# Reordering the opening, the scales and the down weights' unpacking in the first job of a fused FFN, S4, FFN kernel

## The chip, the cores and the metric

The kernel runs on one core of a Trainium2 chip. The core has a matrix engine (TensorE, PE in the profile), a vector engine (VectorE, DVE), a scalar engine (ScalarE, ACT), GpSimd (POOL) and SyncE (SP), which here only issues transfers (DMAs). Each engine has its own list of instructions and works it off in order; engines wait for each other through semaphores. The metric is the device time of one execution in microseconds (us), lower is better: the median of several executions.

## The reference

The input is 2048 tokens of width HID = 1024, as (2, 1024, 1024). Three residual layers follow each other, each after a layer norm: half of an FFN, an S4 convolution along the sequence, and half of the same FFN once more.

```python
def _dequant(qweight, scales, qzeros, g_idx):
    shifts = jnp.arange(PACK, dtype=jnp.uint32) * BITS
    qw = qweight.astype(jnp.uint32)
    w = (qw[:, None, :] >> shifts[None, :, None] & MAXQ).reshape(-1, qweight.shape[1])
    qz = qzeros.astype(jnp.uint32)
    z = ((qz[:, :, None] >> shifts[None, None, :] & MAXQ) + 1).reshape(qzeros.shape[0], -1)
    s = scales[g_idx]
    return (w.astype(scales.dtype) - z[g_idx].astype(scales.dtype)) * s
...
xf = x.reshape(-1, x.shape[-1])
h = jax.nn.silu(xf @ Wg) * (xf @ Wu)
out = h @ Wd
...
x = x + 0.5 * ffn(layernorm(x))
x = x + s4(layernorm(x))
x = x + 0.5 * ffn(layernorm(x))
```

Wg and Wu are 1024 x 2752, Wd is 2752 x 1024. All three are stored as 4-bit numbers, eight to a 32-bit word, with one scale and one zero point for every 128 rows (a group) of a column.

## The kernel before

**Jobs.** The tokens are cut into four blocks of 512. A job is one FFN on one block; there are eight (JOBS), and the S4 layer of two blocks is woven into the jobs between. A job has a gate-and-up half (`gate_up`) and a down half (`down`). Only job 0 unpacks weights: it turns the 4-bit words into signed bytes less their zero points, writes these bytes to memory (w_q for gate and up, wd_q for down), and all later jobs read them back.

**Gate and up.** The 21.5 blocks of 128 hidden columns are taken in 8 waves: waves 0 to 4 of three blocks, waves 5 to 7 of two, the last with the half block too. A wave has 8 steps, one for each group g of 128 input rows, so there are 64 steps. A step multiplies one tile of weights by the block's normalised, transposed input. Each product is made twice, with the rounded high part xTh (fp32r) and with the small rest xTl (f16) (L857): 12 matmuls a step in waves 0 to 4, 8 in waves 5 and 6, 10 in wave 7. The sums pg stay in PSUM; between two groups each is multiplied by the quotient of the two groups' scales, rat (`scaled`; ScalarE L813, VectorE L817). So a matmul of group g+1 waits for the rescale of its own sum. After a wave's last group, `gated` makes g = silu (ScalarE L889), hf = up times g (VectorE L892, three buffers in hfpool), and `halves` splits hf into hh and hl (POOL L898, L899). The halves of wave 0 are put off: they are kept in the list `put_off` and taken in wave 1, at g > 4.

**Down.** 44 steps, two halves of 512 output columns with 22 hidden blocks each, 8 matmuls a step (L951), with a rescale between hidden blocks (L813, L817).

**A weight's way in job 0.** `fetch` and `fetch_zeros` load packed words and zero points (SyncE, L563, L570); `split` runs `signed_bytes` on VectorE (L624, L628, L631); `dequantize` copies eight planes out as bytes q (POOL L669, for wave 1 also ScalarE L667); `keep_bytes` stores them (SyncE L675); `load_bytes` reads a step's tile b back (SyncE L774, 4 steps ahead); `make_weights` casts it to w_up (POOL L790, some on ScalarE L788, 3 steps ahead). The down weights go the same way in six blocks (`fetch_down`, `split_down`, `dequantize_down` POOL L703, `keep_bytes_down` SyncE L711, `load_bytes` L781).

**The opening.** The first tile has no time for the way through memory: `first_split` unpacks wave 0, `dequantize_first` writes its eight planes j as bytes q (odd by POOL L605, even by ScalarE L607), and each plane is copied straight into the first tile b (L608). `keep_first` stores the planes to w_q (L612). The zero points of all of gate and up are unpacked into ztab (`zero_points_in_pieces`, L351, L360) and stored as z_dram (L380), from which `fetch_zeros` reads. The first block's rows xn are normalised by `first_rows` (ScalarE L1815, VectorE L1817) and transposed by `first_turn` (TensorE L1830, ScalarE L1832, VectorE L1833; three of eight through POOL L1837, L1838).

**Scales.** `scale_rows` loads rows of scales (SyncE L399); `scales_in_pieces` transposes them (TensorE L414), copies them out (ScalarE L422), makes them safe against zeros (POOL L425 to L427), takes reciprocals (VectorE L429) and multiplies the quotients rat (POOL L433, L434). This is done for blocks 0 to 2 in the opening, 3 to 8, 9 to 14 and from 15 on in the steps that a list gives.

**What sets the order.** Work that doesn't belong to a step's matmuls hangs on hooks: `at(up, s, f)` has f written before the matmuls of step s of gate and up, or in their middle if s ends in .5; `at(dn, d, f)` the same for the down. `in_pieces` hands a sequence's parts to a list of steps. `pinned` and `in_order_of_writing` fix the written order on the engines named; elsewhere a scheduler may shift instructions within what dependencies allow. All of SyncE's transfers are in one list and leave in order.

Of the kernel before, what the change touches and what calls it, by code (L numbers as in the profile page):

```python
# [57 lines left out]
def macaron_s4_kernel(  # L58
# [314 lines left out]
    def zero_points_in_pieces(which, z):  # L373

        p, n = z.shape
        zi, tab = (t2(f"{a}_{which}").bitcast(I32)[:p, : 8 * n] for a in ("zi", "ztab"))
        yield from unpacked_zeros_in_pieces(tab, z, zi)
        yield
        dst, seg = (zd_dram, SEGD) if which else (z_dram, SEG)
        nc.sync.dma_start(dst.rearrange("g (s n) -> (g s) n", s=seg), tab)  # L380

# [202 lines left out]
    def first_split(zq):  # L584
# [15 lines left out]
        def dequantize(j):  # L600
            pair = pairs.setdefault((j % 2, j // 4), t2(f"q_0_{j}").bitcast(I8)[:, : 2 * n])
            q = pair.rearrange("p (a n) -> p a n", a=2)[:, j // 2 % 2, :]
            view = lambda a, dt: a.bitcast(dt).rearrange("p (n k) -> p k n", k=4)[:, j // 2, :]
            if j % 2:
                nc.gpsimd.tensor_copy(q, view(raw, I8))  # L605
            else:
                nc.scalar.activation(q, view(even, U8), AF.Identity, bias=minus_128)  # L607
            nc.sync.dma_start(first_tile[j:P:8], q[: P // 8])  # L608

# [105 lines left out]
    def first_weights(up, dn, at):  # L715
# [17 lines left out]

        def when(n):
            if n < 12:
                return up, s0 + n
            return dn, n - 14 if n >= 24 else n - 12 if n > 15 else (0, 0, 1, 2)[n - 12]

        def soon(n):
            hooks, s = when(n)  # L740
            return hooks, s + 0.5

        for n in range(6 * 8):
            k, j = divmod(n, 8)
            a, rt = divmod(k, 3)
            if j == 0:
                at(*when(max(0, n - 7)), lambda a=a, rt=rt: fetch_down(a, rt))
                steps = [when(max(0, n - d)) for d in (4, 3, 3, 2, 1, 0)]
                if n == 8:
                    steps = [(up, s0 + d) for d in (3.5, 4, 5, 5.5, 6.5, 7.5)]  # L750
                if n == 16:
                    steps = [(dn, d) for d in (1, 1.5, 2, 2.5, 3, 4)]
                in_pieces(at, steps, lambda a=a, rt=rt: split_down(a, rt))
            at(*when(n), lambda a=a, rt=rt, j=j: dequantize_down(a, rt, EVEN_FIRST[j]))
            if j % 2:
                at(*soon(n), lambda a=a, rt=rt, j=j: keep_bytes_down(a, rt, j // 4, j // 2 % 2))

# [25 lines left out]
    def make_weights(i):  # L783
        j, stage, s = queue[i]
        b = loaded.pop(i)
        made[i] = t = wpool.tile(list(b.shape), F32R, tag="w", name=f"w_{stage}_{j}_{s}")
        if j == 0 and stage == "up" and s % GK in ((), (5, 6, 7), (1, 2, 5))[(s > 7) + (s > 23)]:
            nc.scalar.copy(t, b)  # L788
        else:
            nc.gpsimd.tensor_copy(t, b)  # L790
# [28 lines left out]
    def gate_up(j, b, hooks):  # L819
        hi, lo = pieces[b]  # L820
        ps = {}
        for s, (wi, g) in enumerate(STEPS):
            if wi == 1 and g > 4 and put_off:
                put_off.pop(0)()
# [62 lines left out]
    def gated(j, f, pg, pu):  # L887
# [12 lines left out]

        if j == 0 and f in WAVES[0]:
            put_off.append(halves)
# [696 lines left out]
    def fast():  # L1599
# [5 lines left out]
        for j, (b, k) in enumerate(JOBS):  # L1605
# [88 lines left out]
            if j == 0:  # L1694
                rows = {}
                for s, f in ((0, lambda: next(points, None)), (0, lambda: fetch_zeros(1)), (1, lambda: fetch(2)), (2, lambda: fetch_zeros(2))):
                    at(up, s, pinned(f, ET.SP))
                for first_use, s, k0, k1 in ((5, 1, 3, 9), (14, 6, 9, 15), (30, 11, 15, WIDE)):
                    load = lambda k0=k0, k1=k1: rows.update({k0: scale_rows(k0, k1)})
# [8 lines left out]
                for c in range(1, NC):  # L1708
                    more = lambda c=c: first_turn(c)
                    at(up, {1: 0.5, 2: 0.5, 4: 2.5}.get(c, c - 2), pinned(more, *STARTING, ET.PE))  # L1710
                at(up, 1, pinned(lambda: first_rows(2, 512, HID), ET.DVE))
                first_weights(up, dn, at)
# [7 lines left out]
            if after:  # L1720
                ab, ak = after
                if ak == 1:
                    at(up, 55 if j == 0 else 6, lambda: load_x(ab, rows_of(u, ab)))
                    if j == 0:
                        steps = [(dn, 4 + (3 * i) / 2) for i in range(8)] + [(dn, 15.5), (dn, 16)]
                        in_pieces(at, steps, lambda: moments_by_tile(ab, 1, True, LIFT))
                        steps = [(dn, 17 + i / 2) for i in range(10)]
                        in_pieces(at, steps, lambda: deviations_in_pieces(ab, 1))
# [117 lines left out]
    def start():  # L1846
# [21 lines left out]
        dequantize_first(2)  # L1868
        next(second)
        next(first_scales)  # L1870
        guess(0, 1, mv, LIFT)
        for _ in first_scales:
            pass
        keep_first(1, 0, nc.gpsimd)
        dequantize_first(4)
        dequantize_first(6)
        keep_first(0, 0, nc.sync)
        keep_first(1, 1, nc.gpsimd)
        keep_first(0, 1, nc.scalar)
        keep_warm(10, scratch)  # L1880
# [15 lines left out]
        first_rows(3, P, 512)  # L1896
        for t in (0, 1, 3):
            first_rows(t, 512, HID)
        keep_warm(6)
        return points, zeros_down  # L1900

    points, zeros_down = in_order_of_writing(start, *STARTING, ET.PE, ET.Pool)
    x.pop(0)
# [87 lines left out]
```

## Time and profile before

| | us |
|---|---|
| median of 3 executions | 2038.86 (2038.42 to 2038.87) |
| the profiled execution | 2038.82 |
| its span, first to last instruction | 2036.9 |
| first matmul of gate and up, job 0 | starts 19.19 |
| gate and up of job 0 (64 steps) | 19.19 to 191.60 |
| down of job 0 (44 steps) | 191.60 to 280.72 |
| gate and up of job 3 (no unpacking, no S4 work) | 806.67 to 962.26 |
| down of job 3 | 962.26 to 1040.64 |

The profile is of one execution. Times count from the first instruction. An instruction's line gives its start, its length, engine, line of the kernel and operation, with output and input (partitions x elements); at the end in brackets, how long the engine had been idle before it, and who released it. "x3" at the end means three like instructions in a row. SPq, ACTq are instructions that issue transfers. The granted clock (PEclk) is the share of full speed at which TensorE was allowed to run. Since job 3 runs the same matmuls with nothing to unpack, it serves as the measure of job 0's stages. The time of a step is taken from the start of its first matmul to that of the next step's first.

### The profile page before, as it was taken

The numbers are of one execution on the slowest core, as the hardware profiler recorded it, in microseconds if no ns is written. First come the engines' busy times: TensorE is split into PE (matmuls) and PEld (weight loads), VectorE is DVE, ScalarE is ACT, GpSimd is POOL, SyncE is SP. The second block draws the span as 40 slices with busy tenths as digits, with TensorE's granted clock in tenths as the row PEclk, the third lists the DMA queues.
The fourth block names the chain that finished last, engine by engine and source line by source line (L and its number), as shares of the span: only waits on it lengthen the run. The fifth ranks groups of instructions, "written<-read, shape, count | busy, mean of one in ns | idle before, by whom it ended". The sixth has DMA issues, their size and how long they took to land.

```text
span 2036.9 us, 29679 instructions
## 1 busy us (share of the span) xinstructions
PE 2005.1 (98%) x9202; PEld 1373.4 (67%) x9202; DVE 1627.9 (80%) x2710; ACT 1416.2 (70%) x2221; POOL 1372.1 (67%) x1771
## 2 busy tenths in 40 slices
PE   7999999999999999999999999999999999999998
PEld 4555776577766677665876578667686676866576
DVE  8888878868888787878778777887878878777776
ACT  7888787747775576777767776764776646767775
POOL 6878868748765577756976578754687636965542
PEclk9999999999999999999999999999999999999999
DMA  4344332243524227411562126242163331661113
GB/s 159 104 121 132 110 88 76 68 105 85 154 74 98 79 62 202 121 30 35 135 171 83 33 50 169 81 94 82 47 158 98 81 89 39 159 192 36 34 36 103
DMA packets 345965, 197.13 MB, mean 97 GB/s; under 512 B 166989, under 2 KB 323670, under 8 KB 345798
## 3 DMA queue, kind: packets, MB, share of 16 engines
q1 hardware_dynamic: 344382, 192.74, 34.9%
q10 hardware_dynamic: 1288, 2.01, 0.3%
q8 instruction: 75, 1.23, 0.3%
q14 instruction: 92, 0.75, 0.1%
q0 software_dynamic: 128, 0.39, 0.1%
HBM read 127.52 MB, written 48.57 MB: 86 GB/s over the span
## 4 chain that ended last, share of the span: by engine, by line
PE 93%; DVE 3%; ACT 2%; issue 1%; POOL 1%; DMA 1%; SPq 0%; ACTq 0%; DVEq 0%; POOLq 0%
PE pg L857 57%; PE po L951 30%; PE pc L1319 3%; PE pb L1319 1%; ACT pg L813 1%; DVE pg L817 1%; DVE po L817 0%; DVE rawd L628 0%; POOL w_up L790 0%; DMA x<-in_L_attn_u_dram 0%; DVE hf L892 0%; POOL hl L899 0%; DMA b<-wq 0%; POOL hh L898 0%; PE pt L239 0%
## 5 line engine op out<-in xcount | busy, mean ns | idle before, releaser
L813 ACT ACTIVATE pg<-pg,rat 128x512 f32<-128x512 f32 x1280 | 807.0, 661 | 387.1 <-PE pg L857 383.2
L817 DVE TENSOR_TENSOR pg<-pg,rat 128x512 f32<-128x512 f32 x1128 | 747.8, 692 | 150.7 <-PE pg L857 143.8
L857 PE MATMUL pg<-xTh,w_up 128*128 128x512 f32 x2752 | 845.5, 435 | 6.3 <-DVE pg L817 2.5
L857 PE MATMUL pg<-xTl,w_up 128*128 128x512 f16 x2752 | 708.9, 382 | 4.8 <-DVE pg L817 2.4
L857 PEld LDWEIGHTS pg<-xTh,w_up 128*128 128x128 f32 x2752 | 518.7, 189 | 170.4 <-ACT pg L813 6.9
L790 POOL CAST w_up<-b 128x768 fp32r<-128x768 int8 (+2 forms) x491 | 375.3, 770 | 362.5 <-PE pg L857 259.1
L813 ACT ACTIVATE po<-po,ratd 128x512 f32<-128x512 f32 x669 | 437.9, 662 | 143.3 <-PE po L951 142.7
L951 PE MATMUL po<-hl,w_down 128*128 128x512 f32 x1344 | 526.6, 393 | 1.6 <-DVE po L817 1.4
L951 PE MATMUL po<-hh,w_down 128*128 128x512 f32 x1344 | 521.3, 390 | 0.0
L817 DVE TENSOR_TENSOR po<-po,ratd 128x512 f32<-128x512 f32 x611 | 423.7, 696 | 112.8 <-PE po L951 112.3
L857 PEld LDWEIGHTS <-w_up 128*128 128x128 bf16 x2752 | 226.9, 98 | 342.8 <-issue 158.4
L790 POOL CAST w_down<-bd 128x512 fp32r<-128x512 int8 x352 | 219.0, 625 | 145.0 <-PE po L951 71.9
L951 PEld LDWEIGHTS po<-hl,w_down 128*128 128x128 f32 x1344 | 251.9, 188 | 64.5 <-DVE po L817 6.1
L951 PEld LDWEIGHTS po<-hh,w_down 128*128 128x128 f32 x1344 | 252.4, 188 | 50.6
L899 POOL TENSOR_TENSOR hl<-hf,hh 128x512 fp32r<-128x512 f32 x168 | 218.5, 1300 | 6.5
L898 POOL CAST hh<-hf 128x512 fp32r<-128x512 f32 x168 | 107.3, 639 | 81.4 <-DVE hf L892 62.6
L892 DVE SCALAR_TENSOR_TENSOR hf<-pg,rat,g 128x512 f32<-128x512 f32 x168 | 121.0, 746 | 40.5 <-ACT g L889 34.7
L889 ACT ACTIVATE g<-pg,rat 128x512 f32<-128x512 f32 x168 | 110.1, 687 | 33.7 <-PE pg L857 17.5
L1004 POOL TENSOR_TENSOR x<-x,yr 128x512 f32<-128x512 f32 x52 | 66.9, 1286 | 0.0
L291 POOL TENSOR_TENSOR lo<-x,hi 128x512 f16<-128x512 f32 x48 | 62.3, 1298 | 0.0
L189 DVE BATCH_NORM_STATS2 stats<-x 128x6 f32<-128x512 f32 x88 | 59.9, 680 | 0.0
L289 POOL TENSOR_TENSOR mid<-hi,top 128x512 bf16<-128x512 f32 x48 | 56.1, 1169 | 0.0
(214 smaller groups left out, 1079.2 us busy)
## 6 DMA issues: line engine op xcount, KB each, us to landing
b<-wq SPq DMA_DIRECT2D x319, 96.0 KB
bd<-wdq SPq DMA_DIRECT2D x336, 64.0 KB
x<-in_L_attn_u_dram SPq DMA_DIRECT2D x30, 512.0 KB
yz<-y SPq DMA_DIRECT2D x56, 256.0 KB
yr<-yz SPq DMA_DIRECT2D x56, 256.0 KB
b<-wq SPq DMA_DIRECT2D x128, 64.0 KB
sz<-xn SPq DMA_DIRECT2D x16, 512.0 KB
st<-sz SPq DMA_DIRECT2D x64, 128.0 KB
```

Source lines behind the costliest of these rows:

```text
L291: nc.gpsimd.tensor_tensor(lo[:, own], n[:, own], hi[:, own].bitcast(F32), ALU.subtract)
L790: nc.gpsimd.tensor_copy(t, b)
L813: nc.scalar.activation(dst, src, AF.Copy, scale=sc)
L817: nc.vector.tensor_tensor(dst, src, sc.to_broadcast(list(dst.shape)), ALU.mult)
L857: product = lambda: nc.tensor.matmul(p, weights, (lo, hi)[k][:, g, :], start=(g == 0 and not done), stop=(g == GK - 1 and done), skip_grou ...
L889: nc.scalar.activation(g, pg, AF.Silu, scale=rat[:, 2 * f, GK - 1 :])
L892: nc.vector.scalar_tensor_tensor(hf, pu, last, g, ALU.mult, ALU.mult)
L898: nc.gpsimd.tensor_copy(hi, hf)
L899: nc.gpsimd.tensor_tensor(lo, hf, hi.bitcast(F32), ALU.subtract)
L951: nc.tensor.matmul(ps[c], w[:, bass.ts(c, P)], part, start=(f == 0 and k == 0), stop=(f == NF - 1), skip_group_check=True,)
L1004: nc.gpsimd.tensor_tensor(part, part, rows_back.pop((a, t)), ALU.add)
L1319: nc.tensor.matmul(dst, lhsT, rhs, start=start, stop=stop, skip_group_check=True)
```

## The change

1. Opening: the plane j = 6 of the first tile and the table z_dram are sent by ScalarE instead of SyncE, the table at the end of `start` instead of in step 0; both odd planes are stored by POOL before it makes the first quotients; the second half of wave 1's packed words is fetched after the stores of the even planes; the rows xn of tile 2 are normalised within `start` and no longer in step 1.
2. Scales of blocks 3 to 8 are made from step 4 (before: 5), those of blocks 9 to 14 from step 6 (before: 14), with their rows loaded in steps 0 and 1 (before: 1 and 6).
3. `make_weights`: the casts of ScalarE at s % 8 in (1, 2, 5) begin with s > 31 instead of s > 23.
4. The halves of blocks 0 to 8 are put off instead of those of 0 to 2, and taken at g > 4 in waves 1, 2 and 3.
5. The down's six blocks are fetched, split, copied and stored at steps written in one table. A number d is step 52 + d of gate and up below 12, and step d - 12 of the down from there.
6. In the down of job 0, the statistics of the next block's rows and their deviations are taken at other steps.

No instruction is added or removed on any engine; two transfers change the engine that issues them. Jobs 1 to 7 are as before.

```diff
--- before.py
+++ after.py
@@ -376,8 +376,8 @@
         zi, tab = (t2(f"{a}_{which}").bitcast(I32)[:p, : 8 * n] for a in ("zi", "ztab"))
         yield from unpacked_zeros_in_pieces(tab, z, zi)
         yield
-        dst, seg = (zd_dram, SEGD) if which else (z_dram, SEG)
-        nc.sync.dma_start(dst.rearrange("g (s n) -> (g s) n", s=seg), tab)
+        dst, seg, queue = (zd_dram, SEGD, nc.sync) if which else (z_dram, SEG, nc.scalar)
+        queue.dma_start(dst.rearrange("g (s n) -> (g s) n", s=seg), tab)
 
     def inverse(*what):
         for _ in inverse_in_pieces(*what):
@@ -605,7 +605,8 @@
                 nc.gpsimd.tensor_copy(q, view(raw, I8))
             else:
                 nc.scalar.activation(q, view(even, U8), AF.Identity, bias=minus_128)
-            nc.sync.dma_start(first_tile[j:P:8], q[: P // 8])
+            queue = nc.scalar if j == 6 else nc.sync
+            queue.dma_start(first_tile[j:P:8], q[: P // 8])
 
         def keep(odd, half, queue):
             rows = w_q[0].rearrange("(r b a two) n -> two b r a n", b=2, a=2, two=2)[odd, half]
@@ -731,29 +732,26 @@
                 at(up, s0 + o, lambda w=w, odd=odd: keep_bytes(w, odd))
         s0 = len(STEPS) - 12
 
-        def when(n):
-            if n < 12:
-                return up, s0 + n
-            return dn, n - 14 if n >= 24 else n - 12 if n > 15 else (0, 0, 1, 2)[n - 12]
-
-        def soon(n):
-            hooks, s = when(n)
-            return hooks, s + 0.5
-
-        for n in range(6 * 8):
-            k, j = divmod(n, 8)
+        def when(d):
+            return (up, s0 + d) if d < 12 else (dn, d - 12)
+
+        blocks = (
+            (-3, (-1, -0.5, 0, 0.5, 1, 1.5), (1, 1, 2, 3, 4, 5, 6, 7)),
+            (1, (3.5, 4, 5, 5.5, 6.5, 7.5), (8, 9, 10, 11, 12, 12, 13, 14)),
+            (9, (13.5, 15, 16.5, 17.5, 19, 19.5), (18, 18, 18.5, 19, 20, 20, 21, 21.5)),
+            (15, (20.5, 22, 23.5, 24, 25, 25.5), (24.5, 24.5, 25, 25.5, 26, 26.5, 27, 27.5)),
+            (22, (27, 28.5, 30, 31, 31.5, 32.5), (31.5, 31.5, 32, 32.5, 33, 33.5, 34, 34.5)),
+            (29, (35, 37, 39, 39.5, 41, 41.5), (40, 40.5, 41, 41.5, 42, 42.5, 43, 43.5)),
+        )
+        for k, (fetched, split_at, copied) in enumerate(blocks):
             a, rt = divmod(k, 3)
-            if j == 0:
-                at(*when(max(0, n - 7)), lambda a=a, rt=rt: fetch_down(a, rt))
-                steps = [when(max(0, n - d)) for d in (4, 3, 3, 2, 1, 0)]
-                if n == 8:
-                    steps = [(up, s0 + d) for d in (3.5, 4, 5, 5.5, 6.5, 7.5)]
-                if n == 16:
-                    steps = [(dn, d) for d in (1, 1.5, 2, 2.5, 3, 4)]
-                in_pieces(at, steps, lambda a=a, rt=rt: split_down(a, rt))
-            at(*when(n), lambda a=a, rt=rt, j=j: dequantize_down(a, rt, EVEN_FIRST[j]))
-            if j % 2:
-                at(*soon(n), lambda a=a, rt=rt, j=j: keep_bytes_down(a, rt, j // 4, j // 2 % 2))
+            at(*when(fetched), lambda a=a, rt=rt: fetch_down(a, rt))
+            in_pieces(at, [when(d) for d in split_at], lambda a=a, rt=rt: split_down(a, rt))
+            for i, (j, d) in enumerate(zip(EVEN_FIRST, copied)):
+                at(*when(d), lambda a=a, rt=rt, j=j: dequantize_down(a, rt, j))
+                if i % 2:
+                    half = lambda a=a, rt=rt, i=i: keep_bytes_down(a, rt, i // 4, i // 2 % 2)
+                    at(*when(d + 0.5), half)
 
 
     LOAD, MAKE = 4, 3
@@ -784,7 +782,7 @@
         j, stage, s = queue[i]
         b = loaded.pop(i)
         made[i] = t = wpool.tile(list(b.shape), F32R, tag="w", name=f"w_{stage}_{j}_{s}")
-        if j == 0 and stage == "up" and s % GK in ((), (5, 6, 7), (1, 2, 5))[(s > 7) + (s > 23)]:
+        if j == 0 and stage == "up" and s % GK in ((), (5, 6, 7), (1, 2, 5))[(s > 7) + (s > 31)]:
             nc.scalar.copy(t, b)
         else:
             nc.gpsimd.tensor_copy(t, b)
@@ -820,7 +818,7 @@
         hi, lo = pieces[b]
         ps = {}
         for s, (wi, g) in enumerate(STEPS):
-            if wi == 1 and g > 4 and put_off:
+            if wi in (1, 2, 3) and g > 4 and put_off:
                 put_off.pop(0)()
             if j == 0 and s < 8:
                 w = in_order_of_writing(next_weights, ET.SP)
@@ -898,7 +896,7 @@
             nc.gpsimd.tensor_copy(hi, hf)
             nc.gpsimd.tensor_tensor(lo, hf, hi.bitcast(F32), ALU.subtract)
 
-        if j == 0 and f in WAVES[0]:
+        if j == 0 and f < WAVES[3][0]:
             put_off.append(halves)
         else:
             halves()
@@ -1693,9 +1691,9 @@
                         at(up, 13 + t, pinned(lambda t=t: store(t), ET.SP))
             if j == 0:
                 rows = {}
-                for s, f in ((0, lambda: next(points, None)), (0, lambda: fetch_zeros(1)), (1, lambda: fetch(2)), (2, lambda: fetch_zeros(2))):
+                for s, f in ((0, lambda: fetch_zeros(1)), (1, lambda: fetch(2)), (2, lambda: fetch_zeros(2))):
                     at(up, s, pinned(f, ET.SP))
-                for first_use, s, k0, k1 in ((5, 1, 3, 9), (14, 6, 9, 15), (30, 11, 15, WIDE)):
+                for first_use, s, k0, k1 in ((4, 0, 3, 9), (6, 1, 9, 15), (30, 11, 15, WIDE)):
                     load = lambda k0=k0, k1=k1: rows.update({k0: scale_rows(k0, k1)})
                     at(up, s, lambda load=load: in_order_of_writing(load, ET.SP))
                     steps = [(up, first_use + i / 2) for i in range(4)]
@@ -1708,7 +1706,6 @@
                 for c in range(1, NC):
                     more = lambda c=c: first_turn(c)
                     at(up, {1: 0.5, 2: 0.5, 4: 2.5}.get(c, c - 2), pinned(more, *STARTING, ET.PE))
-                at(up, 1, pinned(lambda: first_rows(2, 512, HID), ET.DVE))
                 first_weights(up, dn, at)
             if j == 1:
                 tables = s4_tables()
@@ -1722,9 +1719,9 @@
                 if ak == 1:
                     at(up, 55 if j == 0 else 6, lambda: load_x(ab, rows_of(u, ab)))
                     if j == 0:
-                        steps = [(dn, 4 + (3 * i) / 2) for i in range(8)] + [(dn, 15.5), (dn, 16)]
+                        steps = [(dn, d) for d in (2.5, 4, 6, 9, 10.5, 14.5, 16, 17.5, 18.5)]
                         in_pieces(at, steps, lambda: moments_by_tile(ab, 1, True, LIFT))
-                        steps = [(dn, 17 + i / 2) for i in range(10)]
+                        steps = [(dn, 21 + i / 2) for i in range(4)]
                         in_pieces(at, steps, lambda: deviations_in_pieces(ab, 1))
                     else:
                         steps = [(up, s) for s in range(12, 21)] + [(up, 20.5)]
@@ -1866,17 +1863,17 @@
         first_scales = scales_in_pieces(0, 3, srow)
         next(first_scales)
         dequantize_first(2)
-        next(second)
         next(first_scales)
         guess(0, 1, mv, LIFT)
+        for _ in range(2):
+            keep_first(1, _, nc.gpsimd)
+        dequantize_first(4)
+        dequantize_first(6)
+        keep_first(0, 1, nc.scalar)
+        keep_first(0, 0, nc.sync)
+        next(second)
         for _ in first_scales:
             pass
-        keep_first(1, 0, nc.gpsimd)
-        dequantize_first(4)
-        dequantize_first(6)
-        keep_first(0, 0, nc.sync)
-        keep_first(1, 1, nc.gpsimd)
-        keep_first(0, 1, nc.scalar)
         keep_warm(10, scratch)
         keep_warm(10, scratch)
         bias = small.tile([P, NT], F32, tag="bias", name="bias")
@@ -1894,12 +1891,14 @@
         for _ in range(5):
             next(points)
         first_rows(3, P, 512)
-        for t in (0, 1, 3):
+        for t in range(NT):
             first_rows(t, 512, HID)
+        for _ in points:
+            pass
         keep_warm(6)
-        return points, zeros_down
-
-    points, zeros_down = in_order_of_writing(start, *STARTING, ET.PE, ET.Pool)
+        return zeros_down
+
+    zeros_down = in_order_of_writing(start, *STARTING, ET.PE, ET.Pool)
     x.pop(0)
     fast()
     x.clear()
```

## The prediction

> **What bounds the kernel now.** I read the busy table first, then the slices, then the matmuls' windows stage by stage, then the waits and the timeline where a stage is longer than its twin.
>
> ```profile
> span 2036.9 us, 29679 instructions
> PE 2005.1 (98%) x9202; PEld 1373.4 (67%) x9202; DVE 1627.9 (80%) x2710; ACT 1416.2 (70%) x2221; POOL 1372.1 (67%) x1771
> PE   7999999999999999999999999999999999999998
> ```
>
> TensorE is busy for 98% of the span, and no matmul is removed; only its idle or slow time can be won. The change touches job 0 alone, so its stages are set against job 3, which issues the same matmuls without unpacking weights. Columns: stretch, its length, PE busy, granted clock, DMA share, GB/s. The first five rows are job 0's waves 0, 1, 2, 3 and 4, 5 to 7; the sixth is job 3's whole gate and up; the last three are job 0's down in two halves and job 3's down.
>
> ```profile
> 19.19:48.54 29.35, 25.25 (x97) 0.94 0.41 129
> 48.54:71.14 22.60, 22.06 (x98) 1.00 0.48 142
> 71.14:96.32 25.18, 22.54 (x97) 1.00 0.32 100
> 96.32:140.96 44.64, 43.65 (x193) 1.00 0.33 93
> 140.96:191.60 50.64, 49.30 (x208) 1.00 0.52 160
> 806.67:962.26 155.59, 155.36 (x688) 1.00 0.25 75
> ...
> 191.60:234.93 43.33, 41.91 (x169) 1.00 0.36 106
> 234.93:280.72 45.79, 42.99 (x177) 1.00 0.29 87
> 962.26:1040.64 78.38, 78.38 (x344) 1.00 0.55 138
> ```
>
> From the first matmul of one step to that of the next, a clean step of 12 matmuls takes 2.70 us (most steps of the trace), one of 8 takes 1.80, one of 10 takes 2.25; so the five stretches of job 0's waves would take 21.6, 21.6, 21.6, 43.2 and 46.8 (16 x 1.80 + 8 x 2.25) if clean. Excess: 7.8, 1.0, 3.6, 1.4, 3.8 us, 17.6 in all (172.4 against job 3's 155.6 gives 16.8). The down takes 89.1 against 78.4: 10.7, of which some 5 are 48 transposes of about 0.1 us each on TensorE. Before all this lie 19.19 us until the first matmul. What is there to win is some 20 us, 1% of the span. Its sharpest pieces, by single steps and by TensorE's waits:
>
> ```profile
> 15.49 2.66 DMA b<-q
> 18.31 0.83 POOL w_up L790
> 19.19 2.97 PE pg L857 x6
> ...
> 26.35 1.65 DVE L1817 TENSOR_SCALAR xn<-x,mv,r 128x512 f32<-128x512 f32 x1
> 29.12 0.59 PE L857 MATMUL pg<-xTl,w_up 128*128 128x512 f16 x2 [1.17 <-DVE pg L817]
> ...
> 71.21 0.75 DVE L429 RECIPROCAL safe<-safe 128x96 f32<-128x96 f32 x1 [1.71 <-POOL safe L427]
> 73.54 1.15 PE L857 MATMUL pg<-xTh,w_up 128*128 128x512 f32 x3 [0.91 <-DVE hf L892]
> ...
> 86.48 2.22 SPq L774 DMA_DIRECT2D b<-wq  x5
> 88.98 0.83 ACT L788 CAST w_up<-b 128x768 fp32r<-128x768 int8 x1 [2.19 <-PE pg L857]
> 90.42 0.95 PE L857 MATMUL pg<-xTl,w_up 128*128 128x512 f16 x3 [1.53 <-ACT pg L813]
> ```
>
> Read as four stories. (1) The first weights wait for the last plane's copy. (2) Step 2 (4.90 us) stops for a rescale queued behind xn. (3) Step 16 (4.06) stops because VectorE idles 1.71 for the scales' reciprocal while hf waits behind it. (4) Step 21 (4.40) stops because ScalarE waits 2.19 for bytes that SyncE asked for only at 86.48; the first of its stores of q (L675) had begun at 73.54, and each waits for POOL's copies, queued behind the splits hh and hl (0.6 and 1.28 us each).
>
> **What the Trainium skill says.** "SBUF — State Buffer", Terms, has VectorE and GpSimd arbitrate for a shared port pair, an exclusive lock held for the whole instruction. The trace agrees: xn takes 0.54 us at 19.75 and 1.65 at 26.35, beside POOL's xTl (26.43, 1.28). "DMA: Bandwidth & Descriptors", Issuing engines are not separate DMA queues: another issuing engine saves only the sequencer's time. Here that time is 0.5 to 0.6 us an issue, against 2.66 to landing. "TensorE: Matmul & The Clock Gate", Part 1 (the HAM clock gate), lets the clock follow a free-running activity window; wave 0's 0.94 is the trace's half clock, 19.10 to 22.52. Engine queue depths in the same page: ScalarE and VectorE are strict FIFO, as stories 2 to 4 show.
>
> **The change part by part** (gains positive).
>
> Opening. Plane 6 left SyncE at 15.49, because a fetch of raw_1 (0.58, at 14.23) and plane 4 stood ahead; its values were ready at 14.24. Now ScalarE issues it at about 14.3 and SyncE issues plane 4 at 14.23, the fetch coming after the stores. At 2.66 the landing is 16.96 instead of 18.15. POOL must be free: r to 14.5, two store issues 1.70, rat 0.55, so 16.75. First matmul about 18.0, 1.2 earlier. ScalarE's issue of the zero table waits for ztab (19.84) with the first rescale queued behind it; 19.84 + 0.45 = 20.3 against the 20.2 at which that rescale would come: 0.1 lost. The half-clock stretch costs about 1.7 of the 3.4 us. If the window's edge stays at 22.52, up to 0.6 more time is spent at half clock; if the earlier start brings the edge forward, up to 1.5 is won. I take 1.1; bounds 0.5 and 2.5.
>
> Steps 1 to 8. xn of tile 2 goes from step 1 to a place where it takes 0.54 before any rescale: the 1.17 stall goes, and what is late next is the rescale itself; 0.45 to 1.3. Against it, the next scales' chain comes into wave 0: reciprocal 0.75 on VectorE, and on POOL two preparations of 0.3 to 0.4 and two rat of 0.3 to 0.4, with six transposes (0.54 on PE, only moved). VectorE was busy for 10.00 of 10.00 us between 40 and 50, so at step 8 the mirror of story 3 can cost 0.3 to 1.0 or, if its POOL input is early, nothing. Net +0.7; bounds -0.5 and +1.5.
>
> Step 16. The reciprocal and its wait of 1.71 are gone from the border; hf comes straight after its silu. All 1.36 of excess: +1.3 (0.7 to 1.36).
>
> Steps 20 to 24. Halves of blocks 3 to 8 are taken at steps 21 to 23 and 29 to 31 instead of at the wave border, so POOL's q copies come up to six instructions (3 x (0.6 + 1.28) = 5.6 us) earlier, SyncE's stores with them, then the five loads behind them. Casts 25 and 26 also leave ScalarE, and 30 and 31 go to it (0.83 each). The excess of 1.70 at step 21 and 0.5 in 22 and 23: +2.0 (0.8 to 2.2). Its cover: hfpool has three buffers, so hf of the next wave waits for hl of this one, which is now written in the last three steps of the wave.
>
> Blocks of the down. Block 0 spread over up 51 to 53.5: +0.3 (0 to 0.6). Block 2's split used VectorE to the brim in the first four down steps; columns: stretch, its length, VectorE busy:
>
> ```profile
> 191.60:203.00 11.40, 11.26 (x16) 1.00 0.15 41
> 203.00:214.00 11.00, 10.03 (x20) 1.00 0.30 88
> ```
>
> Those steps are 1.91, 2.43, 2.45 and 2.49 instead of 1.82: 2.0 us. The same six pieces (L624, L628, L631; 5.5 us) now lie between steps 1.5 and 7.5, but three statistics (0.68 each) come to steps 2.5 to 6 as well: +1.5 (0.5 to 2.1). Blocks 3 to 5 move by one to seven steps and the deviations from 17 to 21; steps 10 to 20 have an excess of 3.3, largest at 16, 18 and 19 (2.39, 2.62, 2.41) where all these met. VectorE's work stays: +1.0 (0 to 2.5). Steps 22 to 43, where transposes are the excess: 0 (±0.4).
>
> Sum: 1.1 + 0.7 + 1.3 + 2.0 + 0.3 + 1.5 + 1.0 = 7.9. Stalls new to places I have no row for (hf's buffers, step 8) I take at 0.4. Gain 7.5. The profiled execution took 2038.82 (span 2036.9 and 1.9 around it), the median of the runs is 2038.86: the same to 0.04. Forecast 2038.8 - 7.5 = **2031.3**, own range 2028.5 to 2034.
>
> **The rivals.** (a) VectorE is the bound where it matters and its work only moves: the down's and early gains (0.7 + 1.5 + 1.0 + 0.3) vanish, and half a microsecond more in the stretch 40 to 60. Left: 1.1 + 1.3 + 2.0 - 0.5 = 3.9, so 2034.9. For it: 10.00 of 10.00 between 40 and 50. Against it: after 203 VectorE has idle time to take the pieces. (b) Upper bounds meet: 2.5 + 1.5 + 1.36 + 2.2 + 0.6 + 2.1 + 1.5 = 11.8, so 2027.0; the early clock edge decides. (c) Slower: the put-off halves hold hf's three buffers. At steps 24 and 32 the last hf of a wave needs hl popped only one step before; POOL (9.92 busy of 10.00 between 50 and 60) need only be more than about 2 us behind, and VectorE, in order, stops with all rescales behind it, then TensorE without free banks. A backlog of 8 us at each of the two new borders costs 2 x (8 - 2) = 12 us and eats the gain: 2038.8 - 7.5 + 12 = 2043.3. It decides from about 6 us of backlog; against it, wave 1 already worked so, and step 16's stall there was the reciprocal's. (d) The change doesn't reorder what it says: then no change, 2038.8; but the lists are explicit, and it is counted in (a).
>
> **How the numbers follow.** Forecast 0.56, (a) with (d) 0.20 over 2033.5 to 2039, (b) 0.20 over 2025.5 to 2028.5, (c) 0.04. A measurement can tell about 0.2%, 4.1 us, from no change: 2034.8 is the edge. Faster: 0.56 + 0.20 + 0.08 of (a) = 0.84; same 0.12; slower 0.04. The range 2027.3 to 2035.5 leaves out about 0.10 of (b), 0.05 of (a) and (c).
>
> **What would show it.** Right: first gate matmul at about 18.0; step 2 under 4.2; step 16 and step 21 at 2.7 to 3.0; SyncE's loads before step 21 some 5 us earlier; down steps 2 to 4 near 1.9. Wrong: VectorE waiting for POOL's hl before hf at steps 24 and 32; a stall over 1 us at step 8; the half clock lasting beyond 22.5; or statistics bringing the stalls to steps 5 to 8.

## The result, and the profile after

The changed kernel takes 2036.41 us (median of 22 executions, 2031.42 to 2038.60), the kernel before 2039.26 in the same sessions (22 executions, 2037.72 to 2040.71). The ratio over all executions is 0.9983, with a 95% interval of 0.9976 to 0.9989: 3.5 us faster (2.2 to 4.9); the two medians differ by 2.9. Forecast were 7.5 us and a range that ends at 2035.5. The direction was right, the size less than half of what was forecast, and the time lies outside the range. The executions are not evenly spread: 5 of the 22 took 2031.4 to 2033.0, the other 17 took 2035.2 to 2038.6. The profiled one (2036.95) belongs to the upper group; none of the lower group was profiled. The experiments trace the loss to one place in the down of job 0. What puts an execution into one group or the other they leave open.

The page of the changed kernel, span and busy time:

```profile
span 2035.2 us, 29665 instructions
PE 2004.1 (98%) x9202; PEld 1374.5 (68%) x9202; DVE 1631.0 (80%) x2710; ACT 1416.2 (70%) x2221; POOL 1371.5 (67%) x1771
```

Nothing is to be seen there; the stages tell it. The matmuls' windows of the changed kernel (stretch, its length, PE busy, granted clock, DMA share, GB/s), job 0's waves 0, 1, 2, 3 and 4, 5 to 7, then its down cut at steps 21, 30 and 32. (Steps 21 and 43 of the down are the half block and have four matmuls, the others eight.)

```profile
17.85:47.20 29.35, 24.46 (x97) 1.00 0.48 149
47.20:68.88 21.68, 21.68 (x97) 1.00 0.48 138
68.88:90.43 21.55, 21.55 (x98) 1.00 0.34 104
90.43:135.05 44.62, 43.63 (x193) 1.00 0.34 101
135.05:185.34 50.29, 49.08 (x208) 1.00 0.52 162
...
185.34:225.58 40.24, 39.89 (x168) 1.00 0.31 89
225.58:243.16 17.58, 16.82 (x69) 1.00 0.43 124
243.16:252.60 9.44, 5.87 (x17) 0.82 0.18 39
252.60:276.90 24.30, 22.71 (x92) 1.00 0.33 101
```

Waves 1 and 2 have become clean (21.7 and 21.6; they were 22.6 and 25.2). Down step 30 begins at 243.16; before it began at 251.87. Up to there the change had won **8.7 us**, more than the 7.5 forecast for the whole. Then two steps of the down took 9.44 us instead of 4.56, at a granted clock of 0.82. When job 1 began, 3.8 us of gain were left (276.90 against 280.72).

From the start of job 1 to the end the two profiles differ by another 2.1 us (1756.2 before, 1758.3 after), although jobs 1 to 7 have the same instructions; 1.3 of it lie behind the last matmul. The profiles of the experiments below with the same instructions there lie between 1757.3 and 1759.3: the profile of before was at the short end. That is why the spans differ by only 1.7. One profile of the kernel before cannot tell whether it is always shorter there.

The timeline of the changed kernel where the time went:

```profile
243.91 0.61 POOL L704 COPY qd<-rawd 88x512 int8<-88x512 int8 x1
244.01 3.14 DVE L632 TENSOR_SCALAR rawd<-rawd 88x1024 uint16<-88x1024 uint16 x1
244.48 1.27 POOL L259 TENSOR_TENSOR xTl<-turn,xTh 128x512 f16<-128x512 f32 x1
245.71 0.61 POOL L704 COPY qd<-rawd 88x512 int8<-88x512 int8 x1
246.26 1.36 POOL L788 CAST w_down<-bd 128x512 fp32r<-128x512 int8 x2
247.07 0.68 DVE L815 TENSOR_TENSOR po<-po,ratd 128x512 f32<-128x512 f32 x1
247.81 0.50 PE L949 MATMUL po<-hl,w_down 128*128 128x512 f32 x1 [2.47 <-DVE po L815]
249.43 0.63 PE L949 MATMUL po<-hh,w_down 128*128 128x512 f32 x1
```

L632 is the last piece of the last down block's split; the change had moved it from step 26 to 29.5. Undisturbed, the same piece takes 0.41 us. Here it was kept for 3.14, while POOL began and ended three instructions (xTl, qd and the first w_down) and began a fourth. The rescale behind it in VectorE's list began only at 247.07, and TensorE stood for 2.47 us. Soon after the stop the same matmul takes 0.63 us instead of 0.39: the clock had fallen to a half (the granted clock is 0.51 from 248.60 to 252.00). In the Trainium skill, "TensorE: Matmul & The Clock Gate", Part 1, has such a fall follow an idle activity window of some 3.4 us. The trace agrees on the fall to a half, but a stop of 2.47 us, with one of 0.27 a little before, was enough here. A delayed instruction of 0.41 us thus cost 4.9 us.

### The profile page after: what moved, and what is told of

Same layout as the page of the kernel before. It is cut to its first block, busy times and chain, and to the rows that moved or that the text cites. A ratio compares the mean times of both kernels' runs of the same rounds, so it can differ in the third digit from the quotient of the medians.

```text
span 2035.2 us, 29665 instructions
## 1 busy us (share of the span) xinstructions
PE 2004.1 (98%) x9202; PEld 1374.5 (68%) x9202; DVE 1631.0 (80%) x2710; ACT 1416.2 (70%) x2221; POOL 1371.5 (67%) x1771
## 4 chain that ended last, share of the span: by engine, by line
PE 93%; DVE 3%; POOL 1%; issue 1%; ACT 1%; DMA 0%; ACTq 0%; POOLq 0%; DVEq 0%
PE pg L855 58%; PE po L949 30%; PE pc L1317 3%; PE pb L1317 1%; ACT pg L811 1%; DVE pg L815 1%; DVE po L815 0%; POOL w_up L788 0%; DVE rawd L629 0%; POOL r L205 0%; DVE hf L890 0%; POOL hl L897 0%; DVE rawd L632 0%; DVE stats L1797 0%; POOL q L670 0%
## 5 line engine op out<-in xcount | busy, mean ns | idle before, releaser
L855 PEld LDWEIGHTS pg<-xTh,w_up 128*128 128x128 f32 x2752 | 518.4, 189 | 167.5 <-DVE pg L815 7.7
```

Source lines behind the costliest of these rows:

```text
L855: product = lambda: nc.tensor.matmul(p, weights, (lo, hi)[k][:, g, :], start=(g == 0 and not done), stop=(g == GK - 1 and done), skip_grou ...
```

## The experiments

**Is it the place of the last block's split?** First, that split put back to the steps it had before.

```diff
-(29, (35, 37, 39, 39.5, 41, 41.5), (40, ...)),
+(29, (34, 35, 35, 36, 37, 38), (40, ...)),
```

> The changed kernel with the last down block's split back at down steps 22, 23, 23, 24, 25, 26 (its copies as changed). Theory (the piece L632 at step 29.5 is kept off the shared port by POOL's unbroken row of instructions, TensorE stops and its clock halves): steps 30 and 31 fall from 5.21 and 4.22 to 1.9 to 2.7, L632 takes under 0.8 us, and all timed runs lie at 2030.5 to 2033, without the spread of the changed kernel. Rival 1 (VectorE has too much work in that stretch wherever the piece stands): a stall of 2 us or more shows up between steps 22 and 29, time 2034 to 2037. Rival 2 (the spread of the changed kernel comes from the clock of the opening): runs still spread over 2031 to 2038.

Measured: 2034.68 us (10 executions, 2032.56 to 2036.08; ratio 0.9975, 0.9965 to 0.9984). Steps 30 and 31 took 1.92 and 2.63, and L632 0.41 us. But steps 23 and 24 took 3.61 and 3.10 instead of 2.15 and 2.29: the pieces now met the deviations there. The theory's part on step 30 held, rival 1 too: the time was only partly won back, with two of the ten executions below 2033. Another tensor_scalar, x<-x,mv,r, took 2.20 us in step 28, where TensorE didn't stop for it. The clock of the opening, rival 2, is not what put the profiled execution of the changed kernel into the upper group: it ran wave 0 at a granted clock of 1.00.

Second, the kernel before with the last block alone moved to the steps of the change.

> The kernel before with only the last down block moved: fetched at step 17, split at 23 to 29.5, copied at 28 to 31.5, as in the change. Theory: the same stall arises without the rest of the change, L632 takes over 2 us in the profile, steps 30 and 31 lose 3 to 5.6 us, and the time is 2041 to 2045 in most runs. Rival 1 (the stall comes from the other moves, which brought POOL's copies or the statistics there): no stall, 2038 to 2040.

Measured: 2042.52 us (21 executions; ratio 1.0016, 1.0009 to 1.0022), 3.3 us slower than before. This one part of the change is a loss by itself. The theory's stall came at another place: the last piece (L632 of the changed kernel, L631 here) took 1.49, not over 2, and step 30 lost only 0.6; it was another instruction of the same kind that was held, x<-x,mv,r, for 3.43 us in steps 32 and 33, and TensorE stopped for 1.24 behind it.

Third, POOL's turns put off, so that xTl no longer stood in front of L632.

```diff
-at(dn, 26 + 4 * t + 2 * half, piece)
+d = {(0, 1): 30.5, (1, 0): 31.5}.get((t, half), 26 + 4 * t + 2 * half)
+at(dn, d, piece)
```

> The changed kernel with two of POOL's turns of the next block (tile 0, second half; tile 1, first half) put off from down steps 28 and 30 to 30.5 and 31.5, so that POOL has xTh and xTl (0.6 to 1.1 and 1.3 us) no longer in front of L632; VectorE's list is as in the changed kernel. Theory (POOL's row keeps L632 waiting): L632 falls from 3.14 to below 1.5 us, the stop at step 30 falls to under 0.7 us, the clock doesn't halve, 2031 to 2033.5. Rival 1 (VectorE's own work is the cause): step 30 and 31 still lose over 3 us, 2035 to 2037.

Measured: 2037.50 us (10 executions, 2032.47 to 2038.86; ratio 0.9983, 0.9974 to 0.9992). L632 fell to 0.78 as the theory had it, and steps 30 and 31 took 2.50 and 3.07, but the time was not won. Two steps later it happened again, and worse; TensorE stopped in step 33. The timeline of this kernel:

```profile
248.93 4.76 DVE L265 TENSOR_SCALAR x<-x,mv,r 128x512 f32<-128x512 f32 x1
254.94 0.50 PE L949 MATMUL po<-hl,w_down 128*128 128x512 f32 x1 [2.56 <-DVE po L815]
```

Fourth, the last two pieces one step earlier (steps 28 and 28.5).

> The changed kernel with the last two pieces (L629, L632) at down steps 28 and 28.5 instead of 29 and 29.5. Theory: POOL's row (from its wait for bytes, which ended near step 27, to step 31) holds here too, so L632 still takes 1.5 us or more in the profile and part of the loss stays: 2032 to 2036. Rival 1 (a chance meeting of just these two instructions): no stall, 2031 to 2032.5.

Measured: 2034.57 us (8 executions, 2033.52 to 2035.76; ratio 0.9976, 0.9965 to 0.9986). The time lies where the theory had it and above the rival's range, but L632, for which the theory had 1.5 or more, took 0.82, and it was the x<-x,mv,r behind it that took 2.20, at a place where TensorE didn't stop for it. Step 29 took 3.16, with a stop of 0.69 behind VectorE's full list. The long wait moves with the places; it doesn't belong to one pair of instructions. What is common to all: the held instruction is a tensor_scalar with source and result in SBUF, and POOL's xTl runs in front of it or starts within 0.5 us of it.

**Is POOL too full?** Six casts of the down were given to ScalarE, then also the last block's copies spread over steps 28 to 33.

```diff
+elif j == 0 and stage == "down" and s in (29, 31, 33, 35, 37, 39):
+    nc.scalar.copy(t, b)
```

> The changed kernel with the casts of down steps 29, 31, 33, 35, 37 and 39 made by ScalarE instead of POOL; VectorE's list is unchanged. Theory (POOL's row without a pause starves VectorE's tensor_scalar): with 0.6 us less for POOL in every second step its pauses come back sooner; the longest tensor_scalar between down steps 28 and 36 falls from 3.14 to below 2 us and the loss in steps 28 to 34 from 5.6 to below 2.5 us; time 2032 to 2034.5. Rival (VectorE's own work is too much there): loss as before, 2036 to 2038.

> The changed kernel with six casts of the down by ScalarE (steps 29, 31, ... 39) and the last block's copies spread over steps 28 to 33, one about every 0.7 step, as evenly as in the kernel before. Theory (POOL is too full from step 28 to 32, so that its queue runs behind and VectorE's tensor_scalar meets it without pauses): no tensor_scalar above 1.5 us between steps 28 and 36, steps 30 and 31 below 2.0 and 2.7, time 2031.5 to 2033.5. Rival (even a less full POOL keeps one of them waiting): a stop of over 0.7 us remains, 2033 to 2036.

Measured: 2033.36 us (7 executions, ratio 0.9973, 0.9962 to 0.9984) and 2034.07 us (11 executions, ratio 0.9976, 0.9967 to 0.9985). Both are faster, but both still have a tensor_scalar of 2.21 us and a step 30 of 2.85 and 2.87. The longest wait fell from 3.14 to 2.21 us, short of what the theories had asked for (2.0 and 1.5). Giving POOL less to do made the loss smaller, but waits over several of POOL's instructions remained, so load alone doesn't explain them.

**The disputed cost by itself.** In the next kernels VectorE meets a row of POOL's instructions in a bare loop.

> The disputed cost by itself; this kernel computes nothing of the reference. In each stretch VectorE does two rescales from PSUM, one test instruction and another rescale, beside a row of 0, 6 or 14 casts of POOL (128x512, int8 to fp32r, some 0.6 us each) without a pause, and in the last stretches with a pause after the sixth of 14. Theory (a VectorE instruction that needs the shared port gets it only when POOL pauses): tensor_scalar, 0.4 to 0.6 us alone, takes some 3 us beside 6 casts, some 7 to 8 us beside 14, and some 3 us where the row has a pause; rescales from PSUM take 0.7 us in all stretches. Rival (it waits for one POOL instruction at most, as a lock held for the whole instruction would have it): at most 1.2 us in every stretch.

The timeline of that kernel, one stretch:

```profile
14.22 8.05 POOL L148 CAST w<-b 128x512 fp32r<-128x512 int8 x14
15.53 0.70 DVE L125 TENSOR_SCALAR xs<-xs,sc 128x512 f32<-128x512 f32 x1
```

The theory fell. Beside 14 casts without a pause the tensor_scalar takes 0.70 us (0.54 alone): it gets its turn after one of them. Rescales from PSUM (0.70) and statistics (0.68) didn't change beside POOL.

> The disputed cost by itself again, with POOL's instructions of the down as they are there; nothing of the reference is computed. The row of casts alone held a tensor_scalar for one instruction at most (0.70 us beside 14 casts), so the row's length is not the cause. Each stretch has VectorE's rescales from PSUM (1, 2 or 3, to shift the meeting), a tensor_scalar, and a rescale, beside a row of POOL of one of nine mixes of w (cast to w_down), q (strided copy qd), h (xTh) and l (the subtraction xTl). Theory (the two-input xTl on POOL lets the VectorE instruction lose the port, and also against the instructions after it): rows of w, q or h alone cost 1.3 us at most; rows with l before or at the meeting cost 2 us or more. Rival 1 (a change from one kind of instruction to another is enough): the mixed rows cost 2 us or more, the row of l alone doesn't. Rival 2 (the port isn't the cause at all): no stretch above 1.3 us plus one xTl.

The theory of xTl fell too: the longest of 54 tensor_scalars took 1.59 us, no more than one xTl (1.26) and its own time (0.54). This fitted rival 2, that the port was not the cause; the later loops show that these rows only lacked the sequence that makes the wait long. In all long cases of the kernel the small loads of the S4 tables had been on their way, so these came next, in the kernel and in a bare loop.

> The changed kernel with the fourteen small loads of the S4 tables (L1042 to L1050), which the scheduler put into down steps 29 to 33, pinned to the start of job 1; VectorE's and POOL's lists in the down are as in the changed kernel, and the first table work of job 1 starts at step 5 (job 1 may lose some us for it). In every profile with a VectorE instruction of 2 us or more so far, these loads were on their way. Theory (they, not POOL, keep tensor_scalar waiting, or let it lose the port): L632 and the x<-x,mv,r after it stay below 1.7 us, steps 30 and 31 fall to 1.9 to 2.2 and 2.6 to 2.8. Rival (POOL's xTl and the instructions behind it do it without the loads): L632 or the next x<-x,mv,r again takes 2 us or more, steps 30 to 34 lose 2 to 6 us.

> The disputed cost by itself, a third time: rows of POOL as in the down, and beside them nothing (first nine stretches), small loads (next nine), rescales by ScalarE (next nine), matmuls by TensorE (next nine), and all three (last nine); nothing of the reference is computed. Theory (small loads): tensor_scalar takes up to 1.6 us beside nothing, ScalarE or TensorE, and over 2 us in some stretches with loads. Rival 1 (ScalarE's or TensorE's traffic): over 2 us there. Rival 2 (none of these): below 1.7 us in all 45, as in the earlier rows.

Measured in the kernel, with the loads gone from the down: L632 3.14 us again, steps 30 and 31 at 5.16 and 4.23; 2034.93 us (20 executions, 11 at 2033.3 to 2035.0 and 9 at 2036.4 to 2038.3; ratio 0.9978, 0.9971 to 0.9985). The loads are not the cause. The bare loop gave the clue: with nothing beside it, the row q l q w w q (the one that the next expectation calls q l q w w h) held the tensor_scalar for 3.23 us, loads, ScalarE or TensorE beside it changed nothing (3.15 to 3.18), and the row l q w w q h did not hold it (0.95 at most). What the first has at the meeting and the second has not is the copy q, on 88 partitions, ahead of l.

> The disputed cost by itself, a fourth time: the row q l q w w h held a tensor_scalar for 3.2 us, over four of POOL's instructions, whatever else ran; rows of one kind, or with h or w before l, did not. q works on 88 partitions, the others on 128. Capitals change that: Q is q on 128, W, H, L are w, h, l on 88. Nothing of the reference is computed. Theory (a POOL instruction on fewer partitions followed by a longer one on all leaves POOL's lanes out of step, so that the port is never free between two instructions): q l q w w h still about 3.2 us, Q l Q w w Q at most 1.6; W l W w w W about 2 us or more; rows with only Q at most 1.6. Rival (the strided form of q is the cause, whatever its partitions): Q as long as q, W below 1.6.

Two stretches of that kernel's timeline, with q on 88 partitions and on 128:

```profile
9.97 0.61 POOL L159 COPY qd<-words 88x512 int8<-88x512 int8 x1
10.62 3.22 DVE L125 TENSOR_SCALAR xs<-xs,sc 128x512 f32<-128x512 f32 x1
10.63 1.26 POOL L161 TENSOR_TENSOR lo_all<-both,hi_all 128x512 f16<-128x512 f32 x1
11.83 0.61 POOL L159 COPY qd<-words 88x512 int8<-88x512 int8 x1
12.39 1.17 POOL L155 CAST w<-b 128x512 fp32r<-128x512 int8 x2
13.51 0.80 POOL L159 COPY qd<-words 88x512 int8<-88x512 int8 x1
...
34.12 0.61 POOL L167 COPY qd<-words 128x512 int8<-128x512 int8 x1
34.69 1.26 POOL L161 TENSOR_TENSOR lo_all<-both,hi_all 128x512 f16<-128x512 f32 x1
34.76 1.47 DVE L125 TENSOR_SCALAR xs<-xs,sc 128x512 f32<-128x512 f32 x1
35.89 0.81 POOL L167 COPY qd<-words 128x512 int8<-128x512 int8 x1
```

With 88 partitions the tensor_scalar waits over l, q, w and w and gets in before the fifth (the 0.80 of the q at 13.51 shows that one's delay). With 128 it waits for the one that runs. The small difference in the starts is not the reason: in the loop before this one the same row, with q on 88 partitions (and loads beside it), had the tensor_scalar start 0.06 us after l, as here with 128 (0.07), and it was held all the same.

```profile
86.11 1.26 POOL L161 TENSOR_TENSOR lo_all<-both,hi_all 128x512 f16<-128x512 f32 x1
86.17 3.15 DVE L125 TENSOR_SCALAR xs<-xs,sc 128x512 f32<-128x512 f32 x1
```

The plain cast on 88 partitions in place of q held it for 3.12 us in the first of three meetings (0.74 and 1.66 in the others; with q 3.22, 2.40 and 1.67). So in this row the number of partitions decides, not the copy's form. In the 66 meetings of the last three loops with rows on 128 partitions alone the longest tensor_scalar took 1.59 us. One more row did it (w, then l on 88 partitions, then casts on 128: 3.38 us in one of three meetings); a single 88-partition copy followed by l and casts did not (1.51 at most). In the kernels, too, a copy on 88 partitions ran at the start of every tensor_scalar of 2 us or more, or had ended at most 1 us before; away from these copies none of the twelve profiles of a whole kernel has one above 1.65 us.

Then the same remedy in the changed kernel: the copies of the two blocks with 88 rows made on 128 partitions.

```diff
+whole = t4(f"rawd_{a}_{rt}").bitcast(I32)
+if n < P:
+    nc.gpsimd.memset(whole[64:], 0)
...
-unpacked[pair] = qpool.tile([P, 2, 512], I8, tag="q", name=f"qd_{a}_{rt}_{j}")[:n]
+unpacked[pair] = qpool.tile([P, 2, 512], I8, tag="q", name=f"qd_{a}_{rt}_{j}")
```

> The changed kernel with the copies of the two down blocks of 88 rows (blocks 2 and 5) made on all 128 partitions (the lanes beyond 88 hold zeros and are not stored; POOL sets them to zero when the block is fetched, some 0.5 us more for each). Theory (POOL's lanes out of step): no tensor_scalar above 1.7 us in the down, steps 30 and 31 fall to about 1.9 to 2.3 and 2.6 to 2.8, all timed runs at 2030.5 to 2034, median near 2032.5. Rival (POOL's load): L632 or x<-x,mv,r again above 2 us, steps 30 to 34 lose over 2 us, median 2035 to 2037.

Measured: 2033.38 us (8 executions, 2032.59 to 2034.99; ratio 0.9972, 0.9961 to 0.9982). None of the eight reaches the changed kernel's upper group, though the slowest misses it by 0.2 us only. VectorE's timeline, the matmuls' window over steps 30 and 31, and POOL's instructions beside L632:

```profile
244.26 0.79 DVE L632 TENSOR_SCALAR rawd<-rawd 88x1024 uint16<-88x1024 uint16 x1
245.57 0.53 DVE L265 TENSOR_SCALAR x<-x,mv,r 128x512 f32<-128x512 f32 x1
```

```profile
244.44:249.00 4.56, 3.93 (x16) 1.00 0.14 27
```

```profile
243.13 1.64 POOL L710 COPY qd<-rawd 128x512 int8<-128x512 int8 x2
244.72 0.81 POOL L258 CAST xTh<-turn 128x512 fp32r<-128x512 f32 x1
```

The two steps take 4.56 us, exactly as before the change, and the longest tensor_scalar of the down takes 1.24, as the theory had it. But this profile is no clean test. POOL has its instructions in the same order as in the changed kernel, yet L632 met them two places earlier: behind the running copy came xTh, not xTl. And in the run with the scales back (below), whose copies are on 88 partitions, L632 fell beside xTh too and took 0.79 us. The kernel thus escapes the long wait without the remedy when the meeting shifts, and the zeroing added on POOL may have shifted it here. For the remedy speak the bare loop and that none of its eight executions is in the upper group, where 17 of 22 were; that it is the partitions which did it in the kernel is likely, not shown. Its median is the lowest but one of all versions tried, within the noise of the one with six casts by ScalarE (2033.36). Both beat the kernel before; against the changed kernel their intervals overlap (0.9961 to 0.9982 and 0.9976 to 0.9989), and they weren't timed side by side with it.

**Which part cured which stall of gate and up?** The scales put back, then the halves and casts put back, each in the changed kernel.

> The changed kernel with the scales of blocks 3 to 8 and 9 to 14 made where the kernel before makes them (from steps 5 and 14). As the prediction has it: step 16 rises from 2.69 to about 4.0, steps 5 and 6 fall from 3.28 and 3.53 to about 2.75, step 21 stays at 2.7. If step 16 was cured by the put-off halves instead, it stays at 2.7.

> The changed kernel with the halves of blocks 3 to 8 no longer put off and ScalarE's casts as before. As the prediction has it: step 21 rises from 2.69 to about 4.4, steps 22 and 23 to 2.8 and 3.0, step 16 stays at 2.7. If step 21 was cured by the scales having left waves 1 and 2, it stays at 2.7.

The steps' windows, steps 16 and 21, of the kernel with the scales back, then of the one with the halves back:

```profile
69.97:73.79 3.82, 3.16 (x13) 1.00 0.11 36
84.88:87.58 2.70, 2.70 (x14) 1.00 0.67 201
```

```profile
68.80:71.51 2.71, 2.71 (x13) 1.00 0.13 37
82.34:87.06 4.72, 2.87 (x13) 1.00 0.52 144
```

Each stall returns with its own part and not with the other. With the scales back, steps 5 and 6 fall to 2.76 and 2.70 as expected, and steps 9 and 13 rise by 0.96 and 0.57, in step 13 the six transposes among it. Gate and up of job 0 took 167.5 us in the changed kernel, 169.9 with the scales back, 170.1 with the halves and casts back: either part is worth about 2.5 us, by one profile each. The halves and the casts went back together, so which of the two it was is open. The whole times of these two (2035.53 and 2039.26, one execution each) say little, since the first had no long tensor_scalar in its down and the second had one of 3.15 us.

## Why the prediction was right and wrong

**Opening, 1.1 forecast.** Right. The first matmul began at 17.85 instead of 19.19; 18.0 had been forecast. The last plane left ScalarE at 14.52, and the cast started when POOL came free:

```profile
14.52 0.56 ACTq L609 DMA_DIRECT2D b<-q  x1
16.90 0.81 POOL L788 CAST w_up<-b 128x768 fp32r<-128x768 int8 x1
17.85 0.47 PE L855 MATMUL pg<-xTh,w_up 128*128 128x512 f32 x1 [0.17 <-POOL w_up L788]
```

The half clock is gone from wave 0 (1.00 instead of 0.94), but step 0 gained only 0.45. TensorE stood 0.89 at the end of step 0 for VectorE's xTl, which is needed before the next transposes, and step 1 gave 0.57 back.

**Steps 1 to 8, +0.7 forecast.** Too high: from step 0's start to step 8's they and step 0 gave nothing (29.35 in both), so steps 1 to 7 lost the 0.45 of step 0. Step 2 fell from 4.90 to 3.63 as forecast; steps 5 and 6 rose by 1.36. In step 5 it is the six transposes of the second scale chain, which had been in step 13; in step 6 TensorE stood for VectorE's rescale, the stall that the prediction had feared for step 8:

```profile
42.25 0.38 PE L855 MATMUL pg<-xTl,w_up 128*128 128x512 f16 x1 [0.67 <-DVE pg L815]
```

The prediction called the transposes only moved, but left their gain out where they came from: wave 1 won 0.9 that it had not named, 0.57 of it in step 13. Counted together with it, steps 1 to 15 gave +0.5.

**Step 16, 1.3 forecast; steps 20 to 24, 2.0.** Right, by size and cause: 1.37, and 2.27 from step 17 to 23; the two reversals show it. SyncE now asks for the five loads at 78.35, 4.0 us before step 21 begins; before it was 86.48, 0.5 us after. Waves 5 to 7, 0.3 forecast, gave 0.35.

**Down up to step 21, 1.5 and 1.0 forecast.** Steps 0 to 9 gave 1.1 (steps 2 to 4 fell by 1.9, step 8 took 0.7 back), steps 10 to 21 gave 2.0. Sum 3.1 against 2.5. The excess of steps 10 to 20 that the prediction gives as 3.3 is 2.9: a full clean step takes 1.82 us (78.38 us for 344 matmuls in job 3), not the 78.38 / 44 = 1.78 that 3.3 would need.

**The step that failed** is "Steps 22 to 43, where transposes are the excess: 0 (±0.4)". It was -5.5: 44.9 us before, 50.4 after (from 235.85 and 226.50 on). 4.9 of it are steps 30 and 31; 0.6 lie in steps 22 to 29, most of it in 23 and 24. The prediction moved the last block's pieces there at no cost; VectorE seemed to have room in that stretch of the kernel before (busy for 33 of 46 us):

```profile
235.00:281.00 46.00, 32.99 (x51) 1.00 0.29 87
```

But idle time of VectorE was not what these pieces needed. They met POOL, which was then making copies on 88 partitions and turns, and had to wait for it. For such a meeting the prediction carried the one price that its trace showed, xn's 1.65 us for 0.54, one POOL instruction. It named the lock, applied it to xn, and didn't ask where else tensor_scalars were being moved into POOL's work. The Trainium skill, "SBUF — State Buffer", SBUF: two separate sides, says that whichever instruction starts first holds the pair for the whole instruction and the other fully blocks. Measured here, the wait isn't limited to one: in the kernels POOL began and ended two to five further instructions within it, and it took up to 4.76 us. And TensorE's stops behind such waits brought the half clock (stops of 2.28 to 2.56 us in four profiles), which the prediction priced in the opening alone.

Rival (a), VectorE's work only moves, came nearest to the measured time (2034.9) by luck: the gains of the down that it struck out were won (3.1 us up to step 21), and the loss that followed was not the one it named. Rival (b) is summed with 1.5 for blocks 3 to 5, whose own bound is 2.5. Rival (c) expected stops at steps 24 and 32 of gate and up; there are none, they take 2.69 and 2.71. Without the loss in steps 30 and 31 the gain at the start of job 1 would have been 8.7 in this profile.

What stays open: why a POOL instruction on 88 partitions lets the following ones keep the port. That POOL's lanes are then out of step is a reading that fits; no run shows the lanes. Which sequences do it wasn't settled either. That the executions of the upper group are those with the long wait and the half clock is likely: the profiled ones at 2036.95 us here and at 2037.74 and 2038.31 in two experiments have both. But no profile of the changed kernel's lower group exists, and why an execution falls into one or the other is open.

## What to carry to other kernels

Before moving a VectorE instruction into an engine's idle time, look at what it shares with its neighbours: a tensor_scalar from SBUF to SBUF can be held by POOL, a rescale from PSUM wasn't. Price such a meeting by the worst case, including what a TensorE stop of 2.3 us or more did to the clock. When a kernel's times fall into two groups, look in the profile for one instruction that takes several times its usual time, and build its neighbourhood alone.

## What the runs showed of the hardware that was not expected

- A tensor_scalar of 0.54 us beside POOL waited for one instruction at most (0.70 beside casts without a pause, 1.59 with xTl) as long as all of these worked on 128 partitions. In some rows with POOL instructions on 88 partitions it waited for four in a row (3.22 us), for six in one case (3.38 us).
- The same row with its copies on 128 partitions: 1.47 us. A POOL copy of 512 bytes a partition took 0.61 us on 88 partitions and on 128, so the full width cost no time.
- A TensorE stop of 2.47 us was followed by matmuls of 0.63 instead of 0.39 us until about 252. Stops of 2.28 and 2.56 us in two experiments brought the half clock too; one of 1.24 us did not.
